# TensorE operands at other distances in SBUF: spaces ahead of seven tiles of a two-layer graph attention and convolution kernel

## The chip, the cores and the metric

The kernel runs on one core of a Trainium2 chip. The metric is the device time in microseconds (us) of one execution, as the median of several runs. A profile is one execution of the program, recorded by the hardware profiler; its time differs a little from the median, and is given beside its span (from the first to the last recorded instruction).

## The reference

The input `x` has 32 items of 512 rows with 512 features, `adj` is one 512 x 512 matrix of zeros and ones for all of them. Everything is fp32. Two layers follow each other, each of the form layernorm(x + f(x)):

```python
# layer 0: attention with 8 heads of 64, masked by adj
q, k, v = x @ Wq + bq, x @ Wk + bk, x @ Wv + bv           # each 512 x 512 per item
scores = einsum('bihd,bjhd->bhij', q, k) / sqrt(64)
weights = softmax(scores + where(adj == 0, -1e9, 0), axis=-1)
x = layernorm(x + einsum('bhij,bjhd->bihd', weights, v))
# layer 1: graph convolution
y = einsum('nm,bmd->bnd', adj, x)
x = layernorm(x + einsum('bnd,do->bno', y, weight) + bias)
```

## The kernel before

**Matmuls.** A matmul on TensorE has a stationary operand (the weights, here 128 partitions x 128 columns, loaded by an LDWEIGHTS instruction) and a moving operand (128 partitions x 512 columns, streamed past the weights). While one matmul streams, the weights of the next are loaded. Two kinds of number are used. The scores (line 569) and the product of the exponentials with V (line 592) are plain fp32. All other products are made of fp32r operands, one pass each, from numbers that are split into parts: a factor has the parts HIGH, REST and BOTH, and a product of two split matrices takes three passes of four matmuls each (`one_pass`, `three_passes`, lines 397 to 406; the matmul is line 400), HIGH and REST into one PSUM bank and BOTH into another. These products are, per item:

- the projections Q and K (`project`, line 414): 8 units of 12 matmuls; the weights come from a ring of three chunks, `stream` (line 366), which DMA refills from HBM with 768 KB at a time; the moving operand is the split and turned x, the three tiles `factors0`, `factors1`, `factors2` (line 321)
- V (`project_values`, line 436): 4 units of 12; now the weights are slices of the factor tiles, and the moving operand is the tile `wv` (line 848)
- the last product (`convolve`, line 540): 4 units of 12; weights from factor tiles, which then hold the split y, and the moving operand is `w1` (line 868; for the first item `early`, line 703, lies in the same place)
- the product with the adjacency (`aggregate`, line 513, and for the last item `aggregate_rows`, line 534): 32 matmuls; the weights are halves of x (`halves`, in the ring `e` of eight buffers), and the moving operand is `adjT`, the turned adjacency (line 276).

That makes 192 matmuls at line 400 and 32 at line 513 for each of 32 items.

**Order.** The order of the work is written out by hand (`manual_schedule`): `first_half(b)` and `second_half(b)` (lines 762 and 785) interleave the stages of up to three items, so that matmuls of one item run while VectorE (DVE), ScalarE (ACT) and GpSimd (POOL) mask, exponentiate, add, split and normalise another. DVE masks the scores (line 571) and makes the REST parts (line 301), ACT makes exponentials (573), HIGH parts (298) and normalised rows (474), POOL sums the exponentials (584) and makes the BOTH parts (304).

**Places in SBUF.** Tiles come from two pools. `consts` lies first, and holds small constants, `gap` (the mask) and `adjT`. `work` follows, with its tiles in the order in which their names are first asked for: `xin`/`turn`, `e`, `xs`, `attT`, `early`/`w1`, the three factor tiles, `q`, `k`, `wv`, `stream`, `es`, `v` and some small ones. A tile that is first asked for later lies behind, so a longer tile, or a space, moves all tiles behind it. Everything inside these tiles (slices of 128 columns, planes, ring buffers) is at multiples of 512 bytes from the tile's start, but for the 64 columns of a head in `v`, which are 256 bytes.

Of the kernel before, what the change touches and what calls it, by code (L numbers as in the profile page):

```python
# [8 lines left out]
FP = mybir.dt.float32  # L9
FR = mybir.dt.float32r  # L10
# [8 lines left out]
P = 128  # L19
# [143 lines left out]
def gnn_resnorm_kernel(tc, *args):  # L163
    nc = tc.nc
    with tc.tile_pool(name="verdict", bufs=1) as keep:
        verdict = keep.tile([1, 1], I32, name="verdict")
        fast_kernel(tc, verdict, *args)
        amiss = nc.values_load(verdict[0:1, 0:1], min_val=0, max_val=1,
                               skip_runtime_bounds_check_because="it is a comparison's result, 0 or 1")
        with tc.If(amiss > 0):  # L170
            general_kernel(tc, *args)
# [7 lines left out]
HIGH, REST, BOTH = 0, 1, 2  # L179
# [3 lines left out]
def fast_kernel(ctx: ExitStack, tc, verdict, x, adj, Wq, bq, Wk, bk, Wv, bv, W1, b1, out):  # L183
    nc = tc.nc
    B, N, D = x.shape
    H = Wq.shape[1] // HD
    HP = H // 2
    NB = N // P
    DB = D // P
# [3 lines left out]
    consts = ctx.enter_context(tc.tile_pool(name="consts", bufs=1))  # L193
    work = ctx.enter_context(tc.tile_pool(name="work", bufs=2))
# [78 lines left out]
    watched = consts.tile([P, 2, NB, GROUP], FP, name="watched")  # L273
    nc.gpsimd.memset(watched, 0.0)

    adjT = consts.tile([P, NB, N], FR, name="adjT")
    inexact = consts.tile([P, NB], FP, name="inexact")
    gap = consts.tile([P, NB, N], U8, name="gap")

    def adjacency(c):  # L280
        turned = work.tile([P, N], FP, name="attT")
        nc.vector.transpose(turned, adj_s[:, c, :, :].rearrange("p j f -> p (j f)"))
        nc.scalar.activation(adjT[:, c, :], turned, AF.Copy)
        nc.vector.tensor_scalar(gap[:, c, :], turned, 0.0, None, op0=ALU.is_equal)
# [10 lines left out]
    XT, QT, KT, V = {}, {}, {}, {}  # L295
# [10 lines left out]
    def split_weight(high, rest, w):  # L306

        nc.scalar.activation(high, w, AF.Copy, scale=SHRINK / EPSILON)
        nc.vector.scalar_tensor_tensor(rest, w, 1.0 / EPSILON, plain(high), op0=ALU.mult, op1=ALU.subtract)
# [8 lines left out]
        nc.gpsimd.tensor_sub(both, plain(rest), plain(temp))  # L318

    def factors():  # L320
        return [work.tile([P, DB, N], FR, name=f"factors{f}", bufs=1) for f in (HIGH, REST, BOTH)]

    def x_transpose(c):

        if c == 0:
            XT[0] = factors()
        pt = bank(DB, P)
        for d in range(DB):
            nc.tensor.transpose(pt[:, d, :], IN[0, c][:, d * P:(d + 1) * P], ident)
        high, rest = (XT[0][f][:, :, c * P:(c + 1) * P] for f in (HIGH, REST))  # L330
        split_high(high, pt)
        split_rest(rest, high, pt)
# [11 lines left out]
    def split_x(b, d):  # L344

        if d == 0:
            XT[b] = factors()
        high, rest, both = (XT[b][f][:, d, :] for f in range(3))
        a = TURN.pop((b, d))
        split_high(high, a)  # L350
        split_rest(rest, high, a)
        split_both(both, high, rest)
# [12 lines left out]
    def chunk():  # L365
        return work.tile([P, 3, DB, P], FR, name="stream", bufs=AHEAD)

    def make_chunk(n):

        which, m = SEQUENCE[n]  # L370
        if n < DB:
            made = early[:, n, :, :, :]
        elif n < DB + AHEAD:
            made = chunk()
        else:
            made = work.tile([P, 3, DB, P], FR, name="last_chunk", tag="xs", bufs=2)
        MADE[n] = CHUNK[0, which, m] = made
        split_weight(made[:, HIGH, :, :], made[:, REST, :, :], RAW[which, m // 2][:, m % 2, :, :])
# [128 lines left out]
    def aggregate(b, d):  # L507
        if d == 0:
            YT[b] = factors()
        pm = bank(N)  # L510
        parts = [part[:, m, :] for part in (LOWS.pop((b, d)), HIGHS.pop((b, d))) for m in range(NB)]
        for n, part in enumerate(parts):
            nc.tensor.matmul(pm, part, adjT[:, n % NB, :], start=(n == 0), stop=(n == 2 * NB - 1))  # L513
        split_y(b, d, pm)
# [176 lines left out]
    def run(units):  # L691
        for unit in units:
            unit[0](*unit[1:])
# [5 lines left out]
    def stay_warm(times):  # L699
        for _ in range(times):  # L700
            nc.tensor.matmul(pm, still, still, start=True, stop=True)

    early = work.tile([P, DB, 3, DB, P], FR, name="early", tag="w1", bufs=1)
    stay_warm(7)
    x_transpose(0)
    x_both(0, nc.gpsimd)
    make_chunk(0)
    stay_warm(2)
    for c in range(1, NB):
        x_transpose(c)  # L710
        x_both(c, nc.gpsimd if c < NB - 1 else nc.vector)
        stay_warm(1)
    stay_warm(2)
    make_chunk(1)
    finish_chunk(0)
    finish_chunk(1)
# [126 lines left out]
    for n in range(2, 4):  # L843
        make_chunk(n)
        finish_chunk(n)
    run(ends)
    adjacency(0)
    wv = work.tile([P, 3, DB, N], FR, name="wv", bufs=1)
    for n in range(2, len(units)):
        if n + 2 < len(units):  # L850
# [86 lines left out]
```

## Time and profile before

| | us |
|---|---|
| median of 3 runs (2638.69 to 2639.71) | 2639.64 |
| the profiled execution | 2636.07 |
| its span | 2634.3 |
| TensorE busy (matmul records) | 2607.4 |
| DVE busy | 2186.5 |
| POOL busy | 1765.0 |
| ACT busy | 1592.2 |

The granted clock of TensorE was 0.997 of full speed. PE stands for TensorE's matmuls, PEld for its weight loads, L400 for line 400 of the kernel. In the profile a matmul's record begins when it starts and ends some 162 ns after the next one has begun, since its end is modelled: 389 ns of duration at L400 are a pace of about 227 ns. The pace is therefore read from the starts, of matmuls or of weight loads. An fp32 matmul stands as two records.

### The profile page before, as it was taken

How to read it: one execution, taken by the hardware profiler on the slowest of the kernel's cores; microseconds unless marked ns; L12 is line 12 of the kernel's file. 1: busy time of each engine (PE TensorE's matmuls, PEld its weight loads, DVE VectorE, ACT ScalarE, POOL GpSimd, SP SyncE). 2: the span in 40 equal slices, each digit the busy share in tenths (PEclk: the TensorE clock that was granted, in tenths of full speed). 3: DMA queues.
4: the chain of work that ended last, by engine and by line, in shares of the span. 5: the costliest groups of instructions: out<-in, count | busy, mean ns of one | idle time of the engine just before them, and what ended most of it. 6: DMA issues, size and time to landing. Idle time of an engine off the chain costs nothing.

```text
span 2634.3 us, 35500 instructions
## 1 busy us (share of the span) xinstructions
PE 2607.4 (99%) x11326; PEld 1706.5 (65%) x11326; DVE 2186.5 (83%) x3529; ACT 1592.2 (60%) x2618; POOL 1765.0 (67%) x1087
## 2 busy tenths in 40 slices
PE   9999999999999999999999999999999999999997
PEld 6566666666666666666666666666666666666665
DVE  8878888878887888888888878888888888888878
ACT  4456655657556566566675565755656655657564
POOL 4557668666677676676666766666767668666673
PEclk9999999999999999999999999999999999999999
DMA  8666444665445664446644456544466444665411
GB/s 244 170 162 176 141 111 115 170 178 158 111 118 148 178 171 130 111 123 178 178 151 109 119 157 178 163 120 116 137 178 174 145 110 115 169 178 152 120 50 51
DMA packets 674273, 379.42 MB, mean 144 GB/s; under 512 B 586784, under 2 KB 590880, under 8 KB 674080
## 3 DMA queue, kind: packets, MB, share of 16 engines
q1 hardware_dynamic: 673792, 376.56, 52.1%
q8 instruction: 92, 1.51, 0.2%
q14 instruction: 101, 0.83, 0.1%
q10 hardware_dynamic: 288, 0.52, 0.1%
HBM read 302.52 MB, written 74.45 MB: 143 GB/s over the span
## 4 chain that ended last, share of the span: by engine, by line
PE 93%; DVE 3%; DMA 1%; issue 1%; POOL 1%; ACT 1%; SPq 0%; DVEq 0%; POOLq 0%; ACTq 0%
PE bank L400 51%; PE bank L569 17%; PE bank L592 16%; PE bank L513 9%; DMA stream<-kept_k 1%; DVE bnst L459 0%; DVE e L571 0%; POOL es L584 0%; DVE factors L301 0%; PE bank L534 0%; POOL factors L304 0%; DVE part L631 0%; SPq L240 0%; DMA xs<-in_adj_dram 0%; DVE square L625 0%
## 5 line engine op out<-in xcount | busy, mean ns | idle before, releaser
L400 PE MATMUL bank<-factors,stream 128*128 128x512 f32 x3012 | 707.5, 393 | 5.8 <-DVE factors L301 1.8
L400 PEld LDWEIGHTS bank<-factors,stream 128*128 128x128 f32 x3012 | 560.3, 188 | 175.5 <-issue 31.9
L584 POOL TENSOR_TENSOR es<-e 128x1024 f32<-128x1024 f32 x128 | 306.8, 2397 | 512.6 <-ACT e L573 512.6
L584 POOL TENSOR_TENSOR es<-es,e 128x1024 f32<-128x1024 f32 x256 | 614.2, 2399 | 20.1
L571 DVE SCALAR_TENSOR_TENSOR e<-gap,bank 128x512 f32<-128x512 uint8 x1024 | 617.3, 678 | 6.0 <-PE bank L569 5.9
L573 ACT ACTIVATE e<-e 128x1024 f32<-128x1024 f32 x512 | 509.9, 1050 | 43.8 <-DVE e L571 27.2
L304 POOL TENSOR_TENSOR factors<-factors,factors 128x512 fp32r<-128x512 f32 x253 | 359.6, 1436 | 201.6 <-DVE factors L301 201.2
L569 PE MATMUL bank<-q,k 64*128 64x512 f32 x2048 | 476.7, 600 | 0.9 <-DVE q L412 0.9
L592 PE MATMUL bank<-e,v 128*64 128x512 f32 x2048 | 453.6, 595 | 0.0
L569 PEld LDWEIGHTS bank<-q,k 64*128 64x128 f32 x2048 | 218.2, 186 | 229.9 <-issue 152.0
L400 PE MATMUL bank<-w,factors 128*128 128x512 f32 x1536 | 360.4, 393 | 1.8 <-DVE factors L301 1.5
L663 ACT ACTIVATE rows<-rows,zero,inverse 128x64 f32<-128x64 f32 x992 | 340.9, 426 | 31.2 <-POOL es L584 22.3
L298 ACT ACTIVATE factors<-bank 128x512 fp32r<-128x512 f32 x132 | 78.5, 597 | 462.8 <-PE bank L513 459.9
L400 PE MATMUL bank<-wv,factors 128*128 128x512 f32 x1536 | 357.8, 392 | 0.0
L400 PEld LDWEIGHTS bank<-w,factors 128*128 128x128 f32 x1536 | 285.3, 188 | 86.1 <-ACT e L573 22.7
L400 PEld LDWEIGHTS bank<-wv,factors 128*128 128x128 f32 x1536 | 285.8, 188 | 84.8 <-ACT xs L474 24.3
L592 PEld LDWEIGHTS bank<-e,v 128*64 128x64 f32 x2048 | 141.4, 137 | 278.4 <-issue 276.6
L513 PE MATMUL bank<-adjT,halves 128*128 128x512 f32 x960 | 229.6, 396 | 0.0
L474 ACT ACTIVATE xs<-xs,shift,rstd 128x512 f32<-128x512 f32 x248 | 184.1, 804 | 48.4 <-DVE shift L469 48.4
L513 PEld LDWEIGHTS bank<-adjT,halves 128*128 128x128 f32 x960 | 180.8, 188 | 43.6
L411 ACT ACTIVATE q<-bank,bq_c 128x512 f32<-128x512 f32 x128 | 87.0, 679 | 194.4 <-PE bank L400 194.4
L491 POOL TENSOR_TENSOR halves<-xs,halves 128x512 fp32r<-128x512 f32 x120 | 151.8, 1298 | 62.1 <-ACT halves L487 62.1
(101 smaller groups left out, 2504.8 us busy)
## 6 DMA issues: line engine op xcount, KB each, us to landing
stream<-kept_q SPq DMA_DIRECT2D x124, 768.0 KB, 6.0
stream<-kept_k SPq DMA_DIRECT2D x124, 768.0 KB, 4.9
xin<-in_x_dram SPq DMA_DIRECT2D x496, 64.0 KB, 2.8
turned<-attT SPq DMA_DIRECT2D x124, 256.0 KB, 2.3
rows<-turned SPq DMA_DIRECT2D x496, 64.0 KB, 3.7
xs<-in_x_dram SPq DMA_DIRECT2D x31, 1024.0 KB, 7.0
out_dram<-xs SPq DMA_DIRECT2D x31, 1024.0 KB, 5.4
part<-passed SPq DMA_DIRECT2D x256, 8.0 KB, 3.3
```

Source lines behind the costliest of these rows:

```text
L304: engine.tensor_sub(both, plain(high), plain(rest))
L400: nc.tensor.matmul(pm, left(f, d), right(f, d), start=(f != REST and d == 0), stop=(f != HIGH and d == DB - 1))
L411: nc.scalar.activation(t, near, AF.Identity, bias=bias[:, m:m + 1], scale=1.0 + EPSILON)
L474: nc.scalar.activation(row, row, AF.Identity, bias=SHIFT[t][:, slot:slot + 1], scale=RSTD[t][:, slot:slot + 1])
L491: nc.gpsimd.tensor_sub(low, cols, plain(high))
L513: nc.tensor.matmul(pm, part, adjT[:, n % NB, :], start=(n == 0), stop=(n == 2 * NB - 1))
L569: nc.tensor.matmul(ps[s], keys[:, j * P:(j + 1) * P], queries, start=True, stop=True)
L571: nc.vector.scalar_tensor_tensor(e[:, s, :], gap[:, j, :], NEG * root, ps[s], op0=ALU.mult, op1=ALU.add)
L573: nc.scalar.activation(e, e, AF.Exp, scale=1.0 / root)
L584: nc.gpsimd.tensor_add(ES[b, hp], ES[b, hp] if j > 1 else E[b, hp, 0], E[b, hp, j])
L592: nc.tensor.matmul(po[s * HD:(s + 1) * HD, :], V[b, j][:, h * HD:(h + 1) * HD], e[:, s, :], start=(j == 0), stop=(j == NB - 1))
L663: nc.scalar.activation(part, part, AF.Identity, bias=zero, scale=inverse[:, c, s:s + 1])
```

## The change

The change makes no instruction and takes none away. It asks the `work` pool for seven tiles that nothing writes or reads, ahead of `adjT`, `early`/`w1`, each of the factor tiles, `wv` and `stream`; and `adjT` comes from `work` instead of `consts`.

```diff
-    adjT = consts.tile([P, NB, N], FR, name="adjT")
+    def space(name, words):
+        work.tile([P, words], FP, name=name, bufs=1)
+
+    space("space_adj", 16)
+    adjT = work.tile([P, NB, N], FR, name="adjT", bufs=1)
...
     def factors():
-        return [work.tile([P, DB, N], FR, name=f"factors{f}", bufs=1) for f in (HIGH, REST, BOTH)]
+        tiles = []
+        for f, words in ((HIGH, 16), (REST, 32), (BOTH, 8)):
+            if len(XT) == 0:
+                space(f"space{f}", words)
+            tiles.append(work.tile([P, DB, N], FR, name=f"factors{f}", bufs=1))
+        return tiles
...
         elif n < DB + AHEAD:
+            if n == DB:
+                space("space_stream", 56)
             made = chunk()
...
+    space("space_w1", 16)
     early = work.tile([P, DB, 3, DB, P], FR, name="early", tag="w1", bufs=1)
...
+    space("space_wv", 40)
     wv = work.tile([P, 3, DB, N], FR, name="wv", bufs=1)
```

A word is 4 bytes. The built programs have these start addresses in each partition, here as what remains when they are divided by 512:

| tile | before | after |
|---|---|---|
| e (halves) | 32 | 32 |
| adjT | 448 | 96 |
| early, w1 | 32 | 160 |
| factors0, factors1, factors2 | 32, 32, 32 | 224, 352, 384 |
| q, k | 32, 32 | 384, 384 |
| wv | 32 | 32 |
| stream | 32 | 256 |
| v | 32 | 256 |

From the moving operand of one matmul to the weights that are loaded meanwhile, for the next one, the distance is then (remainder by 512 bytes):

| matmuls | count | moving, weights | before | after |
|---|---|---|---|---|
| L400, projections | 3072 | factors0/1/2, stream (early at first) | 0, 0, 0 | 32, 416, 384 |
| L400, V | 1536 | wv, factors0/1/2 | 0, 0, 0 | 192, 320, 352 |
| L400, last product | 1536 | w1, factors0/1/2 | 0, 0, 0 | 64, 192, 224 |
| L513, L534 | 1024 | adjT, halves | 96 | 448 |
| L569 (fp32) | 1024 | q, k | 0 | 0 |
| L592 (fp32) | 1024 | e, v | 0 and 256 | 224 and 480 |

## The prediction

> **What bounds the kernel now.** I read the page's header and engine shares first, then the list of waits of TensorE, then the timeline of single stretches, and last the chain of waits.
>
> ```profile
> span 2634.3 us, 35500 instructions
> PE 2607.4 (99%) x11326; PEld 1706.5 (65%) x11326; DVE 2186.5 (83%) x3529; ACT 1592.2 (60%) x2618; POOL 1765.0 (67%) x1087
> ...
> PEclk9999999999999999999999999999999999999999
> ...
> PE 93%; DVE 3%; DMA 1%; issue 1%; POOL 1%; ACT 1%; SPq 0%; DVEq 0%; POOLq 0%; ACTq 0%
> PE bank L400 51%; PE bank L569 17%; PE bank L592 16%; PE bank L513 9%; DMA stream<-kept_k 1%; DVE bnst L459 0%; DVE e L571 0%; POOL es L584 0%; DVE factors L301 0%; PE bank L534 0%; POOL factors L304 0%; DVE part L631 0%; SPq L240 0%; DMA xs<-in_adj_dram 0%; DVE square L625 0%
> ```
>
> TensorE is busy for 99% of the span and holds 93% of the chain that ends last; its granted clock was 0.997. The waits of PE for another engine, added up over the span, are under 20 us, and the longest entries are these:
>
> ```profile
> PE bank L534 <- DVE xs L546: 3.3, 2, 1.9
> PE bank L400 <- DVE factors L301: 3.3, 4, 1.2
> ```
>
> So the time is the number of matmuls times their pace, and pace is the only thing that this change can touch: it adds no instruction, and in the two built programs every engine has the same instructions in the same order with the same waits. The pace is read from weight loads, one per matmul, in the timeline (start, duration of the merged group, then xcount):
>
> ```profile
> 1061.93 2.23 PEld L400 LDWEIGHTS bank<-wv,factors 128*128 128x128 f32 x10
> ...
> 1071.95 2.06 PEld L513 LDWEIGHTS bank<-adjT,halves 128*128 128x128 f32 x9
> ...
> 1000.02 0.19 PEld L569 LDWEIGHTS bank<-q,k 64*128 64x128 f32 x2 [0.23 <-issue]
> 1000.45 0.19 PEld L569 LDWEIGHTS bank<-q,k 64*128 64x128 f32 x2 [0.23 <-issue]
> 1000.88 0.19 PEld L569 LDWEIGHTS bank<-q,k 64*128 64x128 f32 x2 [0.23 <-issue]
> ```
>
> A load takes 0.188 us, so ten loads in 2.23 us are (2230 - 188) / 9 = 226.9 ns apart, nine in 2.06 us (2060 - 188) / 8 = 234.0 ns. Both are one fp32r matmul of 512 columns with a 128x128 weight tile, without any wait inside. Over the whole trace the steady start-to-start distance at L400 is 226.67 ns (5106 of 6014 neighbours are 226 to 227.9 ns). At L513 the same seven values return in turn, between 231 and 238 ns, with a mean of 234.1 ns. That regularity is no noise: the pace depends on something that is the same in every batch. What differs between the two lines is where the operands lie. While a matmul streams its moving operand, the next one's weights are loaded: at L400 their start addresses differ by a multiple of 512 bytes, at L513 by 96 bytes more than one. The fp32 matmuls of L569 are slower in all but show how little a weight load can cost: each stands as two records, a pair begins every 0.43 us, so a record of 512 columns takes 215 ns.
>
> **The change part by part.** (1) The spaces and the move of the turned adjacency cost no instruction and no transfer. Everything between them shifts by multiples of 32 bytes; DVE, ACT, POOL and the DMA queues do the same work, and with the DMA engines about half busy a changed start of a 6 KB row has cover. I take zero. If DVE were slowed by it, it has 17% of idle time in the span.
>
> (2) L400, 6144 matmuls. The distances from the moving operand to the next weights, by remainder of 512 bytes, go from 0 everywhere to 32, 416 and 384 (projections, factor tiles against the ring), 192, 320 and 352 (values) and 64, 192 and 224 (last product). No row of the trace has any of these. Bounds: below, the 215 ns of the fp32 records, 11.7 ns less than now, so 6144 x 11.7 = 71.9 us gained; above, the 234.1 ns of L513, the only other distance seen, 7.4 ns more, so 45.5 us lost. Within L400 itself, the first matmuls after a switch from fp32 run through 236, 228, 232, 231 ns before they settle, and 18 spacings are below 226, at the least 224 ns. So 226.67 is a value that this distance settles into, and not a floor of the instruction. I take the middle between it and 215, 220.8 ns, because at a remainder of 0 both streams walk the same low addresses, and the fp32 matmuls, which take two records and 0.43 us for one moving operand and so have twice the time to read it, do without the 11.7 ns: these look like reads that get in each other's way, of which distances can spare some. That is an inference from three rows, and the half is a choice. 6144 x 5.9 = 36.2 us gained.
>
> (3) L513 and L534, 1024 matmuls: remainder 96 becomes 448. Bounds: 215 ns, 19.6 us gained; 238 ns, the worst of its seven values, 4.0 us lost. With the same 220.8 ns, 1024 x 13.3 = 13.6 us gained.
>
> (4) L569 keeps a remainder of 0, so zero. L592 goes from 0 and 256 to 224 and 480. Its records are fp32; the even heads stand at 0 and the odd ones at 256, and both show 423 ns between pairs, so I take zero; the bound is 7.4 ns on each of 2048 records, 15.2 us, on either side.
>
> (5) What is late next. Over one batch of 80.77 us in the middle DVE is busy for 67.3 us, POOL for 55.6; a batch that is 1.6 us shorter still has room, but seams exist: weight loads of L400 waited 25.0 us for the masking of scores (L571), 24.3 us for L474 and 22.7 us for L573. Where TensorE comes earlier to a seam, the wait grows by as much. About 72 us of 2634 are such seams beside loads; I give a tenth of the gain back, 5 us.
>
> Sum: -36.2 - 13.6 + 5 = -44.8 us. The profiled execution took 2636.07 us, its span 2634.3 and 1.8 outside it; it lies 3.6 us under the median of the runs, 2639.64. So 2591.3 for a profiled execution and 2594.8 us for the median.
>
> One rule speaks against the change. The Trainium skill, "TensorE: Matmul & The Clock Gate", section "Step-by-step: what each phase is for", says that TensorE has two independent read ports, and that loading the next weights steals no read bandwidth from the running matmul. By it, distances would not matter and the sum would be zero. The rows above do not fit it: 226.9 against 234.0 ns for the same instruction form.
>
> **The rivals.** *Slower: the distance of 0 is the good one.* It is the only distance in the trace whose pace settles at one value; the only other sample, 96 bytes, never settles and costs 7.4 ns more per matmul. If the new distances behave like that one, L400 loses 45.5 us, and with L513 between nothing and 7.6 us better (234.1 to 226.67) the median is 2677 to 2685; with half of the pairs bad it is about 2655 to 2662. For it: the only measured non-zero distance is worse, and the transients at L400 (228 to 236 ns) are all but a few worse than 226.67. Against it: 224 ns exists, and fp32 shows room below. It decides from a mean pace at L400 above 226.67 + 13.6 / 6.144 = 228.9 ns if L513 gains in full, and from 226.7 if L513 gains nothing.
>
> *All collisions gone.* Every fp32r matmul at 215 ns: -71.9 - 19.6 = -91.5 us, 2548 us, before anything is given back. For it: the fp32 records. Against it: nine different distances would all have to be good ones.
>
> *The change does nothing to the pace.* If only finer or coarser address bits than those moved count (the shifts are multiples of 32 bytes, the remainders differ by 32 to 448), the paces stay at 226.67 and 234.1 and the median at 2639.6. Against it: L513 differs from L400 by just such a shift.
>
> **How the numbers follow.** A measurement of this kernel can tell about 0.2%, 5.3 us. The forecast, part of the collisions gone, gets 0.40, with a range of its own of 2560 to 2630; all collisions gone 0.13; no effect 0.05; slower 0.42, since the one non-zero sample is worse and the changed pairs are six times as many at L400 as at L513. So faster 0.53, same 0.05, slower 0.42. The likeliest single case is the partial gain, 2595 us. The range that should hold the time 8 times in 10 takes in most of both signs: from 2550, near the floor of all collisions gone, to 2675, at which the rival has most of its pairs at 234.1 ns.
>
> **What would show it.** In the changed kernel's timeline, ten weight loads of L400 should span about (9 x 221 + 188) ns = 2.18 us instead of 2.23, and nine of L513 (8 x 221 + 188) = 1.96 instead of 2.06; the loads of L569 should still come in pairs 0.43 us apart. If the three groups of L400 (ring, values, last product) show different paces, distances count one by one, and the sum is to be made by group. The forecast is wrong if the loads of L400 span 2.23 us or more, if L592 changes its 0.43 us per pair, or if the pace falls and the span does not, with longer waits of L400 for L571, L301 or L474 in the list of waits.

## The result, and the profile after

| | before | after |
|---|---|---|
| median of 4 runs each, us | 2639.16 (2638.17 to 2639.71) | 2661.16 (2659.61 to 2661.83) |
| the profiled execution, us | 2636.07 | 2661.83 |
| its span, us | 2634.3 | 2660.1 |

The changed kernel is slower by 22.0 us, ratio 1.0082 (95% interval 1.0067 to 1.0097). The prediction had 2595 us. The time lies where the rival "Slower: the distance of 0 is the good one" put it with half of the pairs bad, 2655 to 2662, though not because half of them are (see below). The granted clock of TensorE was 0.997 in both profiles, so it is not the clock.

In the changed kernel line 400 has become L411, 513 has become L524, 534 L545, 569 L580, 592 L603. The header, the engine shares, the chain and the group of the L411 matmuls from its profile page:

```profile
span 2660.1 us, 35500 instructions
PE 2632.9 (99%) x11326; PEld 1707.9 (64%) x11326; DVE 2186.3 (82%) x3529; ACT 1592.8 (60%) x2618; POOL 1767.8 (66%) x1087
...
PE 95%; DVE 3%; ACT 1%; issue 0%; DMA 0%; SPq 0%; DVEq 0%; ACTq 0%
...
L411 PE MATMUL bank<-factors,stream 128*128 128x512 f32 x3012 | 723.0, 398 | 6.4 <-DVE factors L305 1.7
```

The counts of instructions are those of before. DVE, ACT and POOL are busy for the same time within 2.8 us; only PE has grown, by 25.5 us, nearly as much as the span (25.8). So no other engine became late: TensorE itself is slower. (The two spans differ by more than the medians, since the profiled execution before lies 3.1 us under its median and the one after 0.7 us above.) The two longest waits of PE:

```profile
PE bank L411 <- DVE factors L305: 3.2, 4, 1.2
PE bank L545 <- DVE xs L557: 3.1, 2, 1.7
```

They were 3.3 and 3.3 us before: no new wait has come. The timeline of the weight loads (start, duration of the merged group, then xcount), first ten of the projections (the group `factors,stream`), ten of V (`wv,factors`), ten of the product with the adjacency, then the fp32 scores:

```profile
1060.04 2.29 PEld L411 LDWEIGHTS bank<-factors,stream 128*128 128x128 f32 x10
...
1071.92 2.28 PEld L411 LDWEIGHTS bank<-wv,factors 128*128 128x128 f32 x10
...
1083.93 2.25 PEld L524 LDWEIGHTS bank<-adjT,halves 128*128 128x128 f32 x10
...
1089.34 0.19 PEld L580 LDWEIGHTS bank<-q,k 64*128 64x128 f32 x2 [0.23 <-issue]
1089.77 0.19 PEld L580 LDWEIGHTS bank<-q,k 64*128 64x128 f32 x2 [0.23 <-issue]
```

Ten loads of L411 take 2.29 and 2.28 us where ten of L400 took 2.23: (2290 - 188) / 9 = 233.6 ns apart instead of 226.9. Ten of L524 in 2.25 us are 229.1 ns apart, where L513 had 234.0. The fp32 pairs still come every 0.43 us. Over the whole trace, counting starts less than 260 ns apart:

| mean start to start, ns | before | after | change x matmuls |
|---|---|---|---|
| L400 / L411 | 227.3 | 232.7 | +5.4 x 6144 = +33.2 us |
| L513 and L534 / L524 and L545 | 234.1 | 228.9 | -5.2 x 1024 = -5.3 us |
| pairs of L569, and of L592 (median) | 429, 429 | 429, 429 | 0 |

The sum is +27.9 us. With the long starts counted in, all starts that follow one another within L400 and within L411 add up to 1401.3 and 1430.8 us (+29.5), within L513 and L524 to 226.1 and 220.9 (-5.2), within L534 and L545 to 10.7 and 12.1 (+1.4). That is 25.7 of the 25.8 us between the two spans. The step from +33.2 to +29.5 is a smaller number of pauses: 177 starts more than 300 ns apart at L411, 194 at L400. The versions below do not tie that number to the pace: with the same slow pace it is 207 in one of them and 180 in another.

One item shows the same in whole groups. Before, with the last product (`w,factors`), one of the two halves of the projections, V, and the adjacency:

```profile
1085.44 10.76 PEld L400 LDWEIGHTS bank<-w,factors 128*128 128x128 f32 x48 [0.76 <-ACT e L573]
...
1122.23 10.75 PEld L400 LDWEIGHTS bank<-factors,stream 128*128 128x128 f32 x48 [0.76 <-DVE e L571]
1140.35 10.75 PEld L400 LDWEIGHTS bank<-wv,factors 128*128 128x128 f32 x48 [0.81 <-ACT xs L474]
1151.14 7.44 PEld L513 LDWEIGHTS bank<-adjT,halves 128*128 128x128 f32 x32
```

and after:

```profile
1095.69 11.03 PEld L411 LDWEIGHTS bank<-w,factors 128*128 128x128 f32 x48 [0.76 <-ACT e L584]
1114.09 11.01 PEld L411 LDWEIGHTS bank<-factors,stream 128*128 128x128 f32 x48 [0.81 <-issue]
1132.84 11.01 PEld L411 LDWEIGHTS bank<-factors,stream 128*128 128x128 f32 x48 [0.76 <-DVE e L582]
1151.24 10.96 PEld L411 LDWEIGHTS bank<-wv,factors 128*128 128x128 f32 x48 [0.81 <-ACT halves L498]
1162.24 7.29 PEld L524 LDWEIGHTS bank<-adjT,halves 128*128 128x128 f32 x32
```

Four groups are 0.27, 0.26, 0.26 and 0.21 us longer, the adjacency is 0.15 shorter; the waits in brackets ahead of the groups are the same 0.76 and 0.81 us. That is +0.85 us per item (the projections have two halves), 27 us for 32 items.

### The profile page after: what moved, and what is told of

The parts are those of the page before. It is cut to its first block, busy times and chain, and to the rows that moved or that the text cites. A ratio compares the mean times of both kernels' runs of the same rounds, so it can differ in the third digit from the quotient of the medians.

```text
span 2660.1 us, 35500 instructions
## 1 busy us (share of the span) xinstructions
PE 2632.9 (99%) x11326; PEld 1707.9 (64%) x11326; DVE 2186.3 (82%) x3529; ACT 1592.8 (60%) x2618; POOL 1767.8 (66%) x1087
## 4 chain that ended last, share of the span: by engine, by line
PE 95%; DVE 3%; ACT 1%; issue 0%; DMA 0%; SPq 0%; DVEq 0%; ACTq 0%
PE bank L411 52%; PE bank L580 17%; PE bank L603 16%; PE bank L524 8%; DVE factors L305 1%; DVE bnst L470 0%; DVE e L582 0%; PE bank L545 0%; DVE part L642 0%; SPq L232 0%; DMA stream<-kept_k 0%; ACT rows L674 0%; DVE e L639 0%; DMA xin<-in_x_dram 0%; PE bank L712 0%
## 5 line engine op out<-in xcount | busy, mean ns | idle before, releaser
L411 PE MATMUL bank<-factors,stream 128*128 128x512 f32 x3012 | 723.0, 398 | 6.4 <-DVE factors L305 1.7
L411 PEld LDWEIGHTS bank<-factors,stream 128*128 128x128 f32 x3012 | 561.1, 188 | 189.6 <-issue 27.5
L582 DVE SCALAR_TENSOR_TENSOR e<-gap,bank 128x512 f32<-128x512 uint8 x1024 | 617.5, 681 | 6.5 <-PE bank L580 6.5
L584 ACT ACTIVATE e<-e 128x1024 f32<-128x1024 f32 x512 | 509.8, 1050 | 45.7 <-DVE e L582 28.7
L580 PE MATMUL bank<-q,k 64*128 64x512 f32 x2048 | 476.2, 600 | 1.4 <-DVE q L423 0.7
L603 PE MATMUL bank<-e,v 128*64 128x512 f32 x2048 | 453.6, 595 | 0.0
L411 PE MATMUL bank<-w,factors 128*128 128x512 f32 x1536 | 368.7, 398 | 1.7 <-DVE factors L305 1.5
L580 PEld LDWEIGHTS bank<-q,k 64*128 64x128 f32 x2048 | 218.6, 186 | 229.7 <-issue 150.1
L411 PE MATMUL bank<-wv,factors 128*128 128x512 f32 x1536 | 365.0, 396 | 0.0
L411 PEld LDWEIGHTS bank<-w,factors 128*128 128x128 f32 x1536 | 285.4, 188 | 93.7 <-ACT e L584 22.7
L411 PEld LDWEIGHTS bank<-wv,factors 128*128 128x128 f32 x1536 | 285.8, 188 | 91.5 <-ACT halves L498 22.7
L603 PEld LDWEIGHTS bank<-e,v 128*64 128x64 f32 x2048 | 141.4, 137 | 279.2 <-issue 267.2
L524 PE MATMUL bank<-adjT,halves 128*128 128x512 f32 x960 | 224.7, 391 | 0.0
L524 PEld LDWEIGHTS bank<-adjT,halves 128*128 128x128 f32 x960 | 180.3, 188 | 39.6
```

The source lines that it names most:

```text
L411: nc.tensor.matmul(pm, left(f, d), right(f, d), start=(f != REST and d == 0), stop=(f != HIGH and d == DB - 1))
L580: nc.tensor.matmul(ps[s], keys[:, j * P:(j + 1) * P], queries, start=True, stop=True)
L582: nc.vector.scalar_tensor_tensor(e[:, s, :], gap[:, j, :], NEG * root, ps[s], op0=ALU.mult, op1=ALU.add)
L584: nc.scalar.activation(e, e, AF.Exp, scale=1.0 / root)
L603: nc.tensor.matmul(po[s * HD:(s + 1) * HD, :], V[b, j][:, h * HD:(h + 1) * HD], e[:, s, :], start=(j == 0), stop=(j == NB - 1))
```

## The experiments

Each version was compared with runs of the kernel before on the same chip, whose medians were 2637.67 us for the first four kernels below and 2637.47 for the last three.

The theory to be tested after this result: the pace of a 512-column fp32r matmul depends on the distance between its operands alone, 0 is the best distance, and all of the 22 us is that pace. Against it stood that some other distance is better than 0 (then a version with that distance would be faster still); that it is the number or the size of the spaces that costs; and that the adjacency's gain came from its move into the other pool and not from its distance.

**Pace by distance, measured by itself.** The kernel before, with 67 groups of 36 equal matmuls ahead of its work (the bench), the last two of them in bf16, a 2-byte number. The result of these extra matmuls is read by nothing; all else is computed as before.

```diff
+    bench = work.tile([P, 12 * N], FR, name="bench", tag="wv", bufs=1)
...
+    def pace(moving, weights, cols=P, count=N, times=36):
+        for _ in range(times):
+            nc.tensor.matmul(result[0:cols, 0:count], bench[:, weights:weights + cols],
+                             bench[:, moving:moving + count], start=True, stop=True)
...
+    for words in list(range(0, P, 4)) + [0, 1, 2, 3, 5, 6, 7, 127, 126, 125]:
+        pace(0, 1024 + words)
...
```

> The kernel before with 63 groups of 36 equal fp32r matmuls ahead of its work (each group with its own distance from the moving operand to the weights, in steps of 4 to 16 bytes; then groups with both operands shifted together, with the same low distance and other high parts, with 96, 64 and 32 weight columns, with 384 and 256 moving columns, and two groups in bf16); they read one tile that nothing else uses yet, and their results go nowhere. Theory A, the remainder of the distance by 512 bytes decides: the group at 0 settles at 226.7 ns, that at 96 at about 234, the ones at 32 to 448 that the changed kernel has between 228 and 234 ns; both operands shifted together and other high parts stay at 226.7 ns. Theory B, the start address of an operand itself decides (its place within a 32, 64 or 512 byte line): then groups with both shifted change by as much as groups with one shifted. Theory C, neither decides and something else in the long kernel does: all groups at 226.7 ns. If the extra time over 213 to 215 ns is the price of loading weights, it falls with 96, 64 and 32 weight columns, to about 3/4, 1/2 and 1/4 of 12 to 13 ns, and bf16 groups are near 215 ns at both distances. The time of this kernel is longer by about 2300 x 0.23 = 0.5 ms and says nothing else.

The timeline of the weight loads of this kernel, one stretch inside each of six groups: distances of 0, 64, 96, 192 and 256 bytes, and bf16 at 0 bytes:

```profile
12.98 4.50 PEld L712 LDWEIGHTS bank<-bench 128*128 128x128 f32 x20
...
46.21 4.39 PEld L712 LDWEIGHTS bank<-bench 128*128 128x128 f32 x19
...
62.96 4.41 PEld L712 LDWEIGHTS bank<-bench 128*128 128x128 f32 x19
...
113.18 4.31 PEld L712 LDWEIGHTS bank<-bench 128*128 128x128 f32 x19
...
146.36 4.49 PEld L712 LDWEIGHTS bank<-bench 128*128 128x128 f32 x20
...
540.95 4.20 PEld L733 LDWEIGHTS <-bench 128*128 128x128 bf16 x20
```

At 0 the loads are (4500 - 188) / 19 = 226.9 ns apart, at 64 bytes (4390 - 188) / 18 = 233.4, at 96 bytes 234.6, at 192 bytes 229.0, at 256 bytes 226.4. The mean of the last 20 start-to-start distances of each group says it more finely:

| distance, bytes (multiples of 16: the same 256 further) | ns |
|---|---|
| 0, 16, 240 | 226.65 |
| 192 | 228.85 |
| 176 | 230.0 |
| 80 | 232.0 |
| 32, 48, 64, 112, 128, 144, 160, 208, 224 | 233.3 to 233.4 |
| 96 | 234.45 |
| 4, 8, 12 | 232.45, 230.7, 230.0 |
| 20, 24, 28 | 233.35, 230.95, 235.0 |
| 500, 504, 508 | 233.35 |

Each multiple of 16 gives the same with 256 bytes more, to 0.1 ns. (The very first group, at 0, has one stray start; repeated later it gives 226.65.) The same low distance with 512 to 20992 bytes added gives 226.7. No group of 512 fp32r columns settles below 226.65. Moving both operands by 32, 64, 128 or 256 bytes together keeps 226.65 to 226.7, so in steps of 32 bytes it is the distance and not the place; but both shifted by 4, 8 or 16 bytes together give 237.95, 231.1 and 230.0, so the place within 32 bytes counts also. None of the tiles in the table of addresses lies there: all are at multiples of 32. Fewer weight columns don't help (96, 64, 32 columns at a distance of 0: 230.0, 230.2, 231.7), which speaks against a cost that grows with the number of columns to be loaded. bf16 runs at 215.85 ns at a distance of 0 and of 96 bytes alike. So remainders decide the pace, as theory A says, but by 256 bytes and not by 512.

By this table the changed kernel's nine distances give 233.37 for the projections (32, 416, 384), 232.22 for V (192, 320, 352) and 231.85 for the last product (64, 192, 224), and weighted with 3072, 1536 and 1536 matmuls 232.70. Its trace has 232.71. That the totals agree to 0.01 ns is luck: by group the trace has 232.9, 231.8 and 233.3 ns, so the last product is 1.45 ns slower than the table says and the others are about 0.5 faster. In the kernel a distance holds for four matmuls, one pass, and then changes; in the bench it holds for 36.

**The adjacency's space alone, distance 448 there and 0 elsewhere.**

```diff
-    adjT = consts.tile([P, NB, N], FR, name="adjT")
+    def space(name, words):
+        work.tile([P, words], FP, name=name, bufs=1)
+
+    space("space_adj", 16)
+    adjT = work.tile([P, NB, N], FR, name="adjT", bufs=1)
```

> The kernel before with only the adjacency's part of the change: adjT in the working tiles behind a space of 64 bytes, so its distance to the halves is 448 instead of 96; all others keep 0. Theory A: L513 at about 228.8 ns as in the changed kernel, 1024 x 5.3 ns = 5.4 us less than before, 2633.8 us. Theory C (the moved tiles of the other engines or the constants' move cost the time): slower than before, up to the 22 us of the change.

Measured: 2632.79 us against 2637.67, ratio 0.998 (0.9971 to 0.9989), 4.9 us faster. The pace of the adjacency product (line 517 here) is 228.86 ns, that of the whole change; 1024 x (234.1 - 228.9) = 5.3 us. In the timeline:

```profile
1069.96 2.02 PEld L517 LDWEIGHTS bank<-adjT,halves 128*128 128x128 f32 x9
```

Nine loads in 2.02 us are (2020 - 188) / 8 = 229.0 ns apart. So this part of the change is a gain.

**The adjacency without its space, all fp32r distances 0.**

```diff
-    adjT = consts.tile([P, NB, N], FR, name="adjT")
+    adjT = work.tile([P, NB, N], FR, name="adjT", bufs=1)
```

> The kernel before with adjT in the working tiles and no space at all, so that every fp32r distance is 0. Theory A: L513 settles at 226.7 ns, 1024 x 7.4 ns = 7.6 us less than before, 2631.6 us: faster than both kernels. Theory C: as before or slower.

Measured: 2630.0 us, ratio to before 0.9972 (0.9961 to 0.9983). Its adjacency product in the timeline, and its header:

```profile
span 2627.6 us, 35500 instructions
...
1067.58 7.21 PEld L513 LDWEIGHTS bank<-adjT,halves 128*128 128x128 f32 x32
1069.85 2.00 PEld L513 LDWEIGHTS bank<-adjT,halves 128*128 128x128 f32 x9
```

All 32 loads take 7.21 us where before had 7.44; nine in 2.00 us are 226.5 ns apart. 1024 x (234.1 - 226.7) = 7.6 us, and 7.7 were measured. This version is faster than both kernels, by one changed line. The same move into the other pool brings 228.9 ns with a space of 64 bytes and 226.7 without, so the distance sets the pace and not the pool.

**The other six spaces without the adjacency's move.** The diff of the change without its first part; the adjacency stays at 96 bytes.

> The changed kernel with adjT left in the constants: the six other spaces alone. Distances at L400 as in the changed kernel, at L513 96 as before. Theory A: L400 costs its whole 29 us (6014 spacings, 1430.8 against 1401.3 us), L513 nothing: 2639.2 + 29 = 2668 us, and slower than the changed kernel by 5 to 7 us. Theory C: no slower than the changed kernel.

Measured: 2668.3 us, ratio 1.0113 (1.0097 to 1.0128), 30.6 us slower. The mean pace of its three-pass matmuls (line 410 there) is 232.64 ns, that of the adjacency 234.18. Two rows of its timeline:

```profile
1071.26 10.96 PEld L410 LDWEIGHTS bank<-wv,factors 128*128 128x128 f32 x48 [0.81 <-ACT halves L497]
1082.26 7.45 PEld L523 LDWEIGHTS bank<-adjT,halves 128*128 128x128 f32 x32
```

V is as long as in the changed kernel, the adjacency as long as before. The two parts add up within what can be told: 30.6 - 4.9 = 25.7 us, with about 4 us on the first and 2.4 on the second by their intervals, against 22.0 (17.7 to 25.6) for both together.

**Which of the two neighbours decides.** A matmul stands at a distance from its own weights, and at another from the weights that are loaded for the next one. The same bench as above with other groups: operands that alternate between a distance of 0 and of 64, 128 or 192 bytes, other column counts, and plain fp32. All else is computed as before.

```diff
+    for d in (16, 32, 48):
+        pace([(0, W), (d, W + d)])
+        pace([(0, W + d), (d, W)])
+        pace([(0, W), (0, W + d)])
+        pace([(0, W), (d, W)])
+        pace([(0, W + d)] * 4 + [(0, W)] * 4, times=64)
+    for count in (512, 496, 480, 464, 448, 416, 384, 320):
+        for d in (0, 16, 24, 32):
+            pace([(0, W + d)], count=count)
...
```

> The kernel before with 67 further groups of fp32r matmuls (and three of fp32) ahead of its work, on a tile that nothing else uses yet; their results go nowhere. Question: which two reads set the extra time, and what it grows with. Theory D, reads collide while the next weights are loaded: then the distance from a matmul's moving operand to the next matmul's weights counts. Groups that alternate two operands so that each matmul's own distance is 0 and the next one's is 64, 128 or 192 bytes pace at 229 to 234 ns, and groups with the own one at those distances and the next at 0 (mean of both signs) too when the moving operand stays, at about half when every second is at 0; the extra of unaligned distances grows with the time in which load and stream overlap, so it is smaller for fewer weight columns. Theory E, a seam cost at the start of each matmul, set by its own moving operand and its own weights: groups with own distance 0 stay at 226.7 ns whatever the next distance is. In both, the part that aligned distances keep (13.3 ns: 226.7 against 512 columns at 2.4 per ns, 213.3) stays the same for 512 to 320 columns, as 173.3 ns at 384 and 120.0 at 256 did; whether the extra of unaligned distances does is open. The four-by-four groups (four matmuls at a distance, four at 0) tell whether four are enough to settle: 230 to 231 ns if not. fp32 groups of 128 rows: no difference between distances 0, 64 and 96.

The means of the last 24 start-to-start distances of each group:

| pairs, ns | d = 64 | 128 | 192 bytes |
|---|---|---|---|
| own weights at 0, next weights at d or -d | 231.67 | 228.33 | 231.67 |
| own at d or -d, next at 0 | 233.33 | 230.0 | 233.33 |
| moving operand fixed, weights alternate | 232.5 | 232.2 | 230.0 |
| weights fixed, moving operand alternates | 230.8 | 230.0 | 236.7 |

Neither rule holds: if only the distance to the next weights counted, the second row would be at 226.7; if only that to a matmul's own weights, the first would. A pattern of two operands can give a cycle of four values (231, 226, 228, 234 for one of them), so a matmul's time is not fixed by its own operands and the next one's alone. Four matmuls at 64, 128 or 192 bytes and four at 0 in turn give 231.6, 231.7 and 230.0 ns, where two settled halves at 64 bytes would give (233.35 + 226.65) / 2 = 230.0: four in a row do not always settle. And 0 is not the best distance for every shape:

| moving columns | 0 | 64 | 96 | 128 bytes |
|---|---|---|---|---|
| 512 | 226.67 | 233.33 | 234.29 | 232.62 |
| 480 | 216.67 | 215.79 | 217.79 | 213.33 |
| 448 | 206.67 | 202.21 | 200.0 | 203.67 |
| 320 | 146.67 | 146.67 | 146.67 | 146.67 |

Between 512 and 320 columns at a distance of 0 the pace differs by (226.67 - 146.67) / 192 = 0.4167 ns per column, that is 2.4 columns per ns. The least value of each of these rows is columns / 2.4 + 13.33 ns. The expectation that aligned distances keep these 13.3 ns for all counts from 512 to 320 was wrong: at a distance of 0 they have it at 512, 384 and 320 columns, and 15 to 20 ns at the five counts between 512 and 384 that were tried. With 496 and 464 columns none of the four distances came down to 13.33 (the least are 223.33 and 210.0 ns, 16.7 over columns / 2.4). With 112 weight columns instead of 128 the best of 0, 64 and 128 bytes is 64 (226.67, against 228.88 at 0), as if the end of the weights counted; but with 96 columns 128 bytes gives 231.67 and not 226.67, so that is not the whole rule.

The fp32 matmuls of this bench have 128 rows and columns, and two records each, as in the kernel:

```profile
560.02 0.19 PEld L733 LDWEIGHTS bank<-bench 128*128 128x128 f32 x1 [0.24 <-issue]
560.45 0.19 PEld L733 LDWEIGHTS bank<-bench 128*128 128x128 f32 x1 [0.24 <-issue]
```

Their 72 records begin one by one, 429 ns apart, at 0, 64 and 96 bytes alike: such a matmul takes 858 ns. At L569, where a matmul has only 64 rows, two records begin 7 ns apart, and the next two 422 to 423 ns later. So the 0.43 us of a pair is what each record takes, not twice that; which two records make a pair (by the order of the program, those of two heads, on different halves of the partitions) is not shown further.

**All spaces 256 bytes, all fp32r distances 256.** Three spaces of 64 words, ahead of `adjT`, `factors0` and `wv`.

```diff
-    adjT = consts.tile([P, NB, N], FR, name="adjT")
...
+    space("space_adj", 64)
+    adjT = work.tile([P, NB, N], FR, name="adjT", bufs=1)
...
+        for f, words in ((HIGH, 64), (REST, 0), (BOTH, 0)):
...
+    space("space_wv", 64)
```

> The changed kernel with three spaces of 256 bytes (ahead of adjT, factors0 and wv) in place of its seven: all fp32r distances are 256, so the tiles are moved and unwritten spaces stand between them as in the change, but the remainder by 256 is 0. Theory A with a period of 256 bytes: 226.7 ns at L411 and L524, 2630 us, as with adjT at 0 and no space. If spaces or moved tiles in themselves cost the time, or the period is 512: between 2640 and 2668 us.

Measured: 2630.84 us against 2637.47, ratio 0.9974 (0.9964 to 0.9984), as the version with all distances 0.

```profile
1057.24 10.75 PEld L409 LDWEIGHTS bank<-wv,factors 128*128 128x128 f32 x48 [0.81 <-ACT xs L483]
1068.03 7.21 PEld L522 LDWEIGHTS bank<-adjT,halves 128*128 128x128 f32 x32
```

The groups are 10.75 and 7.21 us, those of a distance of 0. So spaces cost nothing in themselves, and the period of 256 bytes holds in the kernel.

**All three-pass distances 64, the adjacency 0.**

```diff
-    adjT = consts.tile([P, NB, N], FR, name="adjT")
...
+    adjT = work.tile([P, NB, N], FR, name="adjT", bufs=1)
...
+        for f, words in ((HIGH, 16), (REST, 0), (BOTH, 0)):
...
+            if n == DB:
+                space("space_stream", 32)
...
+    space("space_wv", 112)
```

> The changed kernel with spaces such that every distance at L411 is 64 (448 for the first item's early weights) and adjT stays at 0: no mixture of distances. The separate pace at 64 bytes is 233.35 ns, so 6144 x 6.7 = 41 us over the kernel with adjT at 0: about 2671 us, more than the changed kernel, whose mixture of nine distances came to 29 us at L411. If the price in the kernel is only that of distances that change from pass to pass, it is less than the change's: 2640 to 2655 us.

Measured: 2664.1 us, ratio 1.0097 (1.0082 to 1.0113). The last two stages of one item:

```profile
1070.90 11.02 PEld L410 LDWEIGHTS bank<-wv,factors 128*128 128x128 f32 x48 [0.81 <-ACT halves L497]
1081.98 7.25 PEld L523 LDWEIGHTS bank<-adjT,halves 128*128 128x128 f32 x32
```

48 loads in 11.02 us instead of 10.75; the mean over the trace is 233.26 ns, the 233.35 of the bench. 6144 x (233.26 - 227.3) - 1024 x (234.1 - 227.4) = 36.6 - 6.9 = 29.7 us, and 26.6 (21.6 to 29.8) were measured. The expected 2671 was too high, since it counted 6.7 ns per matmul from the settled pace at 0; from the mean at 0, which has the first matmuls after each switch in it, there are 6.0. One distance at every tile gives a loss of the same kind as the change's mixture: the remainder at which the pairs stand is enough for it.

## Why the prediction was wrong

The step that failed is (2), the price of L400. It took 220.8 ns, half way between 226.67 and the 215 ns of the fp32 records, and so a gain of 36.2 us; measured are 232.7 ns, and by the means of the trace a loss of 33.2 us. The inference behind it was that 226.67 at a distance of 0 still holds collisions that other distances can spare. The pace by distance shows none: 226.65 is the least of all 41 distances tried. The lower bound of 215 ns was misread. It is half of the 0.43 us from pair to pair at L569, as if the two records of a pair ran one after the other; but they begin 7 ns apart, and where fp32 records begin one by one, in the bench, each takes 429 ns. So no row showed a matmul that does without the 11.7 ns. The 215.85 ns of bf16, measured later, belong to another kind of operand and are no bound for fp32r either. The upper bound, 234.1 ns, was a good one: the worst settled pace at any multiple of 16 bytes is 234.45.

(3) had the right sign and a wrong size: -13.6 us forecast, -5.3 us by the pace, -4.9 us in the run of that part alone. The same assumed 220.8 is the reason; measured is 228.9. Its gain was real, but what it gains is a part of the way back to 226.7, which the distance of 0 gains in full.

(1) and (4) were right. Spaces and the move cost nothing (2630.84 us with three spaces, 2630.0 without any), and the fp32 pairs stay at 429 ns, at L592 too, whose distance changed from 0 and 256 to 224 and 480. The idea of (5), that the waits at the seams move with TensorE, is not shown: TensorE came later, but the weight loads of L411 still waited 25.0 us for the masking (L582) and 22.7 us for the exponentials (L584), as those of L400 did, and the number of pauses did not follow the pace.

The rival was right about the place, L400, and in its claim that 0 is the good distance, and its signs in the profile were the better evidence: 0 was the only distance of that trace whose pace settled at one value, and the one non-zero sample was worse. It said that the change loses if the mean pace at L400 is over 228.9 ns; it is 232.7. Its price for all pairs bad, 2677 to 2685, was too high: it took 7.4 ns per matmul, from 226.67 to 234.1. The mean of before is 227.3, since the first matmuls after each switch from fp32 run above 226.67 there also, and the mean of the nine new distances is 232.7, so the difference is 5.4. Its figure for half of the pairs bad, 2655 to 2662, holds the measured time by luck: by the bench seven of the nine distances are bad ones (233.35 to 234.45 ns) and the other two are in between (228.85).

The rule that was weighed, two independent read ports (the Trainium skill, "TensorE: Matmul & The Clock Gate", section "Step-by-step: what each phase is for"), would have given no change. The fp32r groups disagree with that, 226.65 to 234.45 ns by distance alone; the bf16 groups agree, 215.85 ns at the two distances tried. Whether it is the two reads that get in each other's way in fp32r, no run shows.

What stays open is the mechanism behind the distances. The extra over 13.33 ns depends on both neighbours' distances, on the moving length and on the number of weight columns, in ways that the runs show but no rule tried here covers.

## What to carry to other kernels

When TensorE is busy for 99% of the span, read the pace of each matmul group from the starts, group by group: here two groups of the same shape with different paces, 226.7 and 234.1 ns, differed in their operands' addresses. For fp32r matmuls of 128 weight columns and 512 moving columns, lay all moving and stationary tiles at the same remainder of 256 bytes; here that is one line and 7.7 us of 2638, ratio 0.9972 (0.9961 to 0.9983). Do not take half of a pair of records, or the pace of another data type, as a floor to hope for: measure the pace by itself over the distances first.

## What the runs showed of the hardware

An fp32r matmul of 512 columns never settled below 226.65 ns, 512 / 2.4 + 13.3 ns; 384 and 320 columns at a distance of 0 have the same 13.3 ns over columns / 2.4 (173.3 and 146.67). bf16 has 215.85 ns at 512 columns, 2.5 over 512 / 2.4; a plain fp32 matmul of 128 rows and 512 columns takes two records of 429 ns. The Trainium skill, "TensorE: Matmul & The Clock Gate", section "Step-by-step: what each phase is for", has 215.7 ns from one matmul of 512 columns to the next, which agrees with bf16 and not with fp32r.

The distance acts with a period of 256 bytes, 16 and 240 bytes are as good as 0 (226.65 ns, against 233.35 at 32 and 224), and the best of the values tried moves with the shape: 96 bytes for 448 moving columns (200.0 against 206.67 ns at 0), 128 bytes for 480 (213.33 against 216.67). With 256 moving columns 96 bytes gave 118.65 ns against 120.0 at 0, so 13.3 ns over columns / 2.4 is not a floor for every shape. Both operands 4 bytes past a multiple of 32 cost most of all that were tried with 512 fp32r columns, 237.95 ns at a distance of 0.
